# A decoder block on one core: the queries of five kv groups by seven block products in place of eight

## The chip, the cores and the metric

The kernel runs on one core of a Trainium2 chip. The metric is the device time of one execution in microseconds: the median of three runs is 661.36 us (659.74 to 665.2). Engines are named as in the profile: PE (TensorE, matmuls; PEld its weight loads), DVE (VectorE), ACT (ScalarE), POOL (GpSimd) and SP, whose queue issues all the DMAs.

## The reference

The input `x` is 8 batches of 128 tokens of 512 values. Three blocks follow, each added to `x`; `ln` is a layer norm without weights.

```python
# 32 query heads in 8 kv groups of 4, head size 128, causal
q = (ln(x) @ w_q).reshape(B, S, 8, 4, 128)       # w_q: 512 x 4096
k = (ln(x) @ w_k).reshape(B, S, 8, 128)          # w_k, w_v: 512 x 1024
v = (ln(x) @ w_v).reshape(B, S, 8, 128)
p = softmax(where(causal, einsum("bqhgd,bkhd->bhgqk", q, k) * scale, -inf))
x = x + einsum("bhgqk,bkhd->bqhgd", p, v).reshape(B, S, 4096) @ w_o
# cross attention to a context of 128 rows, whose rows are keys and values
...
# gated feed-forward, 512 -> 1376 -> 512; weights are 4-bit numbers with scales and zeros
x = x + (silu(h @ Wg) * (h @ Wu)) @ Wd           # h = ln(x)
```

## The kernel before

**Numbers.** Almost every operand of a matmul is a pair of F16 tiles, a high part and a remainder. `split` makes them: ACT casts the high part, another engine (DVE from PSUM, POOL from SBUF) subtracts it. A product (`mm3`, lines 158 to 164) is three matmuls: high by high, high by remainder, remainder by high.

**Tiles.** The 1024 tokens are two halves of 512. `hT[part][half]` is ln(x) transposed: four blocks (`k`) of 128 rows of the contraction by 512 tokens. A head's queries for one half are thus 4 x 3 = 12 matmuls of 512 columns into a PSUM bank, `ps_q` (`proj_q`), then split into `qh` and `ql`.

**Steps.** The main loop runs over 64 steps, a kv group `g` and a batch `b` each. A step contains:

- `att_s` of the next step: 12 score matmuls of 64 or 128 columns into `ps_sc` (tag `s`); on DVE four custom reductions that add the mask and find the row maximum; on ACT four exponentials with row sums; then `rec` on DVE and POOL, two scalings of `s` on POOL, the split into `pb` (ACT casts, POOL subtracts), and a transposing DMA `pt<-pb` on SP.
- `proj_piece`: a quarter of the projections of the unit (a group's half) that comes next.
- `att_o` of the step before: 12 matmuls of 512 columns into `ps_o`, added to `xr` by DVE.
- `att_v`: five matmuls of 256 columns into `ps_at` from `pt`, then the split into `ah` and `al`.

**Weights.** They arrive in F32. `fetch_w*` issues the DMA into a raw tile; `sumsq` sums squares on ACT; `scales` makes a scale with a tiny matmul (`ps_n`) and DVE; `convert` multiplies on POOL in place, casts on ACT and subtracts on POOL. A table `todo` says after which step each of these is written.

**Quantized weights.** `nf` are three F16 tiles for the feed-forward weights, filled from step 8 on by `dequant`, in 35 pieces: DMAs of the numbers (`qr`) and of the zeros (`zi`, from a DRAM copy `zd`), two DVE instructions each. The pool `deqp` holds their temporaries, and those of the prologue.

**Order.** `begin` (the prologue) is written in order by hand (`in_order`), as are parts of the tail. In between, the framework's scheduler places the instructions on each engine by its own model; an engine then executes its queue in that order. So which tile waits for which follows from the program, but the order around the change is a result of the build. PSUM has eight banks, two each for the tags `j` (projections), `s`, `a` and `o`.

Of the kernel before, what the change touches and what calls it, by code (L numbers as in the profile page):

```python
# [17 lines left out]
P = 128  # L18
HQ = 64
B = 8  # L20
# [33 lines left out]
def tile_decoder(  # L54
# [34 lines left out]
    masks = []  # L89
    for k in range(2):  # L90
        m = const.tile([P, (k + 1) * HQ], F32, name=f"mask{k}")
        nc.gpsimd.memset(m, 0.0)
        for p0 in (0, HQ):
            part = m[p0 : p0 + HQ, :]
            nc.gpsimd.affine_select(
                part,
                part,
                [[-1, (k + 1) * HQ]],
                ALU.is_ge,
                NEG,  # L100
                base=k * HQ,
                channel_multiplier=1,
            )
        masks.append(m)
# [80 lines left out]
    BANKS = {"j": 2, "s": 2, "a": 2, "o": 2}  # L185
# [9 lines left out]
    qp = pool("q", 5)  # L195
    rawp = pool("raw", 2)
    hp = pool("hT", side="right")
# [18 lines left out]
    def fetch_wq(g, pieces=((0, GH),)):  # L216
        src = wq[:, g * TH : (g + 1) * TH].rearrange("(kt p) d -> p kt d", p=P)
        raw_t["q", g] = raw = rawp.tile([P, KT, TH], F32, name="rawq", tag="rawq", bufs=1)
        for a, b in pieces:
            nc.sync.dma_start(raw[:, :, a * P : b * P], src[:, :, a * P : b * P])  # L220

    def fetch_wk(g):
        raw_t["k", g] = raw = rawp.tile([P, KT, P], F32, name="rawk", tag="rawk")
        nc.sync.dma_start(
            raw, wk[:, g * P : (g + 1) * P].rearrange("(kt p) d -> p kt d", p=P)
        )

    def fetch_wv(pr):
        raw_t["v", pr] = raw = rawp.tile(
            [P, KT, 2 * P], F32, name="rawv", tag="rawv", bufs=1  # L230
        )
        nc.sync.dma_start(
            raw, wv[:, pr * 2 * P : (pr + 1) * 2 * P].rearrange("(kt p) d -> p kt d", p=P)
        )
# [7 lines left out]
    def sumsq(kind, g, i, j, n=1):  # L242

        raw = raw_t[kind, g]
        if kind == "q":
            view = raw[:, :, j * P : (j + 1) * P]
# [11 lines left out]
        junk = work.tile([P, 2 * TH], BF16, name="junk", tag="junk", bufs=1)  # L258
# [105 lines left out]
    def prep_wq(g, j, direct=False):  # L364
# [3 lines left out]
        raw = raw_t["q", g][:, :, j * P : (j + 1) * P]  # L368
# [34 lines left out]

    def ln_stats(b):
# [11 lines left out]
    def ln_apply(b):  # L416
# [3 lines left out]
        h = deqp.tile([P, H], F32, name="h", tag=("qr", "zi")[b % 2], bufs=2)  # L420
# [19 lines left out]
    def h_wide(b):  # L440

        cs = slice(b * P, (b + 1) * P)
        ps = transpose4(ln_t.pop(("h", b)), "s" if b == 2 else "o")
# [15 lines left out]
    def k_wide(g):  # L459
# [13 lines left out]
        wide = h32.rearrange("p k t -> p (k t)")[:, :TH].rearrange("p (b t) -> p b t", b=HB)  # L473
# [5 lines left out]
    def h_dma(b):  # L479
# [3 lines left out]
        hb = deqp.tile([P, 2, H], F16, name="hb", tag="hb", bufs=HB)  # L483
# [16 lines left out]
    def proj_q(g, half, j, pieces=(slice(0, TH),)):  # L500

        ps = bank("j", [P, TH], "ps_q")
        if j % 2 == 0:
            q_t[g, half, j // 2] = [
                qp.tile([P, HB, 2, 2, HQ], F16, name="q" + p, tag="q" + p) for p in "hl"
            ]
        hi, lo = q_t[g, half, j // 2]
        for cs in pieces:
            proj(ps[:, cs], wq_t[g * GH + j], half, cs)
            yield  # L510
        split(
# [3 lines left out]
        )  # L515
        yield
# [12 lines left out]
    def proj_v(pr, b):  # L529
        half, bb = divmod(b, HB)  # L530
        cs = slice(bb * P, (bb + 1) * P)
        ps = bank("j", [P, 2 * P], "ps_v")
# [146 lines left out]
    def scales_load():  # L679

        rows = deqp.tile([SROWS, NFT * P], F16, name="srow", tag="srow")
# [4 lines left out]
        zt["s"] = deqp.tile([P, NFT, SROWS], F16, name="scol", tag="scol")  # L686
# [25 lines left out]
    def inter_scale():  # L712
# [16 lines left out]
        junk = work.tile([P, 2 * TH], BF16, name="junk", tag="junk", bufs=1)  # L729
# [31 lines left out]
    def zeros_load():  # L761
        zw = deqp.tile([NZ, INTER // 8], I32, name="zw", tag="zw")
# [6 lines left out]
    def zeros(es, after):  # L769
        if "z" not in zt:  # L770
            zt["z"] = deqp.tile([NZ, INTER // 8, 8], I32, name="z", tag="z")
# [11 lines left out]
    def zeros_store():  # L783

        zt["d"] = dram.tile([NZ, INTER], I32, name="zd")
        nc.sync.dma_start(zt["d"], zt["z"].rearrange("p a e -> p (a e)"))

    def dequant(m, g, c0, c1, after, pts=None):
# [11 lines left out]
        zi = deqp.tile([P, H], I32, name="zi", tag="zi", bufs=2)  # L800
# [29 lines left out]
    def begin():  # L830

        warm = const.tile([P, TH], BF16, name="warm")
        nc.vector.memset(warm, 0.0)
        psw = bank("s", [P, TH], "ps_w")
# [5 lines left out]
        fill(11)  # L840
# [10 lines left out]
        fetch_wk(1)  # L851
# [79 lines left out]
        prep_wv(0, 1, True)  # L931
        next(q[2])
# [42 lines left out]
    def c_load(b):  # L975
        raw_t["c", b] = c = xc.tile([P, H], F32, name="c", tag="c", bufs=3)
        nc.sync.dma_start(c, cx[b])

    def c_prep(b):
# [3 lines left out]
        cp = xc.tile([P, 2, H], F16, name="cp", tag="cp", bufs=B)  # L983
# [65 lines left out]
    zero = const.tile([P, P], F32, name="zero")  # L1049
    nc.gpsimd.memset(zero, 0.0)  # L1050
# [10 lines left out]
    XC = chunk_steps[-1] + 1  # L1061
# [30 lines left out]

    def h3_load(b):
# [6 lines left out]
    def proj_parts(u, j):  # L1100
# [6 lines left out]
        run(proj_q(g, half, j))  # L1107
        yield
        if projects_v(u) and j in (1, 2):
            for q in range(2):  # L1110
                run(proj_v(g // 2, half * HB + (j - 1) * 2 + q))
# [11 lines left out]
    for g in range(1, NG):  # L1123
        u0 = units.index((g, 0))
        c = HB * (u0 - 2)
        if g > 1:
            m = c - HB
            at(m, lambda g=g: fetch_wk(g))
            at(m + 1, lambda g=g: (fetch_wq(g), sumsq("k", g, 0, 0)))
            at(m + 2, lambda g=g: (sumsq("q", g, 0, 0), sumsq("q", g, 0, 1)))  # L1130
            at(m + 3, lambda g=g: (sumsq("q", g, 0, 2), sumsq("q", g, 0, 3)))
            at(m + 3, lambda g=g: (scales("q", g), scales("k", g), soft_scale(g)))
        for j in range(GH):
            at(c + j, lambda g=g, j=j: prep_wq(g, j))
# [9 lines left out]
        if g % 2 == 0:  # L1144
            c = HB * (u0 - 3)
            at(c - 2, lambda g=g: fetch_wv(g // 2))
            at(c - 1, lambda g=g: sumsq("v", g // 2, 0, 0))
# [337 lines left out]
```

## Time and profile before

| | |
|---|---|
| median of three runs | 661.36 us |
| span of the profiled execution | 659.3 us |
| PE busy | 630.6 us, 96% |
| DVE, ACT, POOL busy | 469.9, 440.4, 395.8 us |
| mean granted TensorE clock | 0.995 |
| DMA | 69.34 MB, mean 105 GB/s |

The profiled execution's own time is known as its span, from the first to the last instruction; it lies within 0.1% of the fastest of the runs, and 2.1 us below their median. PE's busy time is the union of its instructions, which overlap; it doesn't say how many more would fit. Of the loop's 64 steps the profile shows one `rec` on POOL each: from 33.5 us (the first) to 529.1 us (the last). The steps of the groups come before the feed-forward's chains (`ps_c`), which begin among the last attention steps.

### The profile page before, as it was taken

Reading aid. Unit: us, or ns where it says so; the run is one execution under the profiler, and the core shown is the slowest. Engines: PE = TensorE matmul, PEld = TensorE weight load, DVE = VectorE, ACT = ScalarE, POOL = GpSimd, SP = SyncE. Lnnn points to the kernel's source line nnn. Section 1 sums busy time; section 2 is a strip of 40 time slices with the busy share of each in tenths; the row PEclk is TensorE's granted clock in tenths of the full one; section 3 lists DMA queues with packets and bytes.
Section 4 is the critical chain, followed back from the end, with each engine's and each line's share of the span. In section 5 each row is a group of like instructions: output and inputs, shape, how many; then the busy total and the mean of one; then the engine's idle time right before and its main releaser. Section 6 shows DMA issues by size and latency. Waiting matters only on the chain.

```text
span 659.3 us, 12426 instructions
## 1 busy us (share of the span) xinstructions
PE 630.6 (96%) x3992; PEld 341.9 (52%) x3992; DVE 469.9 (71%) x1474; ACT 440.4 (67%) x1238; POOL 395.8 (60%) x586
## 2 busy tenths in 40 slices
PE   8789999899999999999999999899998988999996
PEld 5455545455655555565555565456554444445443
DVE  6845786656767776675778565677776768988986
ACT  5676677465758574666677565976566578867674
POOL 7757497664747795556588597663576247622521
PEclk9999999999999999999999999999999999999998
DMA  9277244945553755455547514242544243112002
GB/s 316 54 174 146 84 46 133 229 105 158 121 157 80 192 130 153 109 152 140 144 112 163 149 37 120 46 103 57 90 76 70 41 86 55 22 27 65 1 1 64
DMA packets 117773, 69.34 MB, mean 105 GB/s; under 512 B 84190, under 2 KB 100593, under 8 KB 117708
## 3 DMA queue, kind: packets, MB, share of 16 engines
q1 hardware_dynamic: 117708, 68.55, 43.7%
q8 instruction: 31, 0.51, 0.3%
q14 instruction: 34, 0.28, 0.1%
HBM read 42.12 MB, written 2.20 MB: 67 GB/s over the span
## 4 chain that ended last, share of the span: by engine, by line
PE 56%; POOL 13%; DMA 10%; DVE 8%; issue 7%; ACT 5%; SPq 1%; DVEq 0%; POOLq 0%; ACTq 0%
PE ps_c L1184 6%; PE ps_c L1185 6%; PE ps_o L164 5%; PE ps_o L162 5%; PE ps_o L163 5%; PE ps_q L163 5%; PE ps_q L162 5%; PE ps_q L164 5%; DMA pt<-pb 3%; DMA rawq<-in_L_attn_w_q_dram 3%; POOL pb L119 3%; DMA rawo<-in_L_attn_w_o_dram 2%; POOL s L625 2%; POOL wql L119 1%; POOL rawo L356 1%
## 5 line engine op out<-in xcount | busy, mean ns | idle before, releaser
L568 ACT ACTIVATE s<-s,negm 128x64 f32<-128x64 f32 (+1 forms) x256 | 93.1, 365 | 31.6 <-DVE negm L611 31.3
L162 PE MATMUL ps_o<-woh,ah 128*128 128x512 f16 x256 | 97.1, 379 | 3.2 <-ACT ah L116 3.2
L162 PE MATMUL ps_q<-hT,wqh 128*128 128x512 f16 (+1 forms) x260 | 98.2, 378 | 1.7 <-DVE ql L119 1.7
L163 PE MATMUL ps_q<-hT,wqh 128*128 128x512 f16 (+1 forms) x260 | 98.2, 378 | 0.0
L164 PE MATMUL ps_q<-hT,wql 128*128 128x512 f16 (+1 forms) x260 | 98.0, 377 | 0.0
L164 PE MATMUL ps_o<-woh,al 128*128 128x512 f16 x256 | 96.9, 379 | 0.6 <-DVE al L119 0.6
L163 PE MATMUL ps_o<-wol,ah 128*128 128x512 f16 x256 | 97.0, 379 | 0.0
L119 POOL TENSOR_TENSOR pb<-s,pb 128x256 f16<-128x256 f32 (+1 forms) x128 | 71.7, 575 | 14.8 <-ACT pb L116 12.4
L665 DVE SCALAR_TENSOR_TENSOR xr<-ps_o,unsc,xr 128x512 f32<-128x512 f32 x64 | 47.8, 747 | 42.5 <-PE ps_o L164 41.9
L611 DVE CUSTOM_DVE_ANT_0 s<-ps_sc,mask,soft 128x64 f32<-128x64 f32 (+1 forms) x256 | 66.9, 309 | 4.3 <-PE ps_sc L164 2.0
L578 POOL TENSOR_SCALAR rec<-rec 128x4 f32<-128x4 f32 x64 | 14.8, 231 | 90.1 <-DVE rec L576 87.4
L625 POOL TENSOR_TENSOR s<-s,rec 128x128 f32<-128x128 f32 (+1 forms) x128 | 64.3, 523 | 4.5
L116 ACT CAST pb<-s 128x256 f16<-128x256 f32 (+1 forms) x128 | 43.0, 350 | 33.7 <-POOL s L625 30.0
L119 DVE TENSOR_TENSOR ql<-ps_q,qh 128x512 f16<-128x512 f32 x64 | 43.9, 686 | 28.8 <-ACT qh L116 28.6
L116 ACT CAST ah<-ps_at 128x512 f16<-128x512 f32 x64 | 37.1, 581 | 23.3 <-PE ps_at L164 10.1
L119 DVE TENSOR_TENSOR al<-ps_at,ah 128x512 f16<-128x512 f32 x64 | 43.7, 683 | 7.0 <-ACT ah L116 6.6
L568 ACT ACTIVATION_READ_ACCUMULATOR s<-s,negm 128x1 f32 x256 | 48.1, 188 | 0.0
L116 ACT CAST qh<-ps_q 128x512 f16<-128x512 f32 x64 | 36.7, 573 | 14.0 <-PE ps_q L164 12.5
L1197 DVE TENSOR_SCALAR ps_c<-ps_c,rTg 128x512 f32<-128x512 f32 (+1 forms) x56 | 40.7, 750 | 7.1 <-PE ps_c L1185 6.8
L356 POOL TENSOR_TENSOR rawo<-rawo,sco 128x512 f32<-128x512 f32 x30 | 31.4, 1053 | 22.5 <-DVE sco L312 20.3
L1195 ACT ACTIVATE ps_c<-ps_c,rTu 128x512 f32<-128x512 f32 (+1 forms) x57 | 36.3, 659 | 11.3 <-PE ps_c L1185 9.2
L164 PE MATMUL ps_sc<-k,ql 128*128 128x64 f16 (+1 forms) x256 | 42.7, 206 | 0.5 <-DVE ql L119 0.5
(243 smaller groups left out, 1728.9 us busy)
## 6 DMA issues: line engine op xcount, KB each, us to landing
rawq<-in_L_attn_w_q_dram SPq DMA_DIRECT2D x8, 1024.0 KB
rawo<-in_L_attn_w_o_dram SPq DMA_DIRECT2D x8, 1024.0 KB, 6.0
zi<-zd SPq DMA_DIRECT2D x26, 256.0 KB, 4.1
vd<-v SPq DMA_DIRECT2D x64, 64.0 KB, 2.6
qr<-_L_ffn_down_qweight_dram SPq DMA_DIRECT2D x10, 256.0 KB
xr<-in_x_dram SPq DMA_DIRECT2D x8, 256.0 KB, 7.7
rawk<-in_L_attn_w_k_dram SPq DMA_DIRECT2D x8, 256.0 KB, 4.5
rawv<-in_L_attn_w_v_dram SPq DMA_DIRECT2D x4, 512.0 KB
```

The lines of the kernel that those rows point to most:

```text
L116: a = nc.scalar.copy(hi, src)
L119: b = (lo_eng or nc.vector).tensor_tensor(lo, src, hi, ALU.subtract)
L162: nc.tensor.matmul(ps, lh, rh, start=start and i == 0, stop=False)
L163: nc.tensor.matmul(ps, lh, rl, start=False, stop=False)
L164: nc.tensor.matmul(ps, ll, rh, start=False, stop=stop and i == n - 1)
L568: exp = nc.scalar.activation(v, v, AF.Exp, bias=negm[:, j : j + 1], scale=-1.0, accum_out=sums[:, j : j + 1],)
L611: nc.vector.tensor_tensor_reduce(view, flat(ps, cols[j]), masks[j // 2], soft_t[g][:, j % 2 : j % 2 + 1], BIG, ALU.add, ALU.min, negm,)
L625: mul = nc.gpsimd.tensor_tensor(v, v, rec[:, 2 * k : 2 * k + 2].unsqueeze(2).to_broadcast([P, 2, (k + 1) * HQ]), ALU.mult,)
L665: return nc.vector.scalar_tensor_tensor(xr[b], ps, unsc_t[g], xr[b], ALU.mult, ALU.add)
L1184: nc.tensor.matmul(ps, lh, rh, start=r == 0, stop=False, skip_group_check=r > 0)
L1185: nc.tensor.matmul(ps, lh, rl, start=False, stop=True, skip_group_check=r > 0)
L1197: nc.vector.tensor_scalar(ps, ps, sc, None, ALU.mult)
```

## The change

The queries of kv groups 2 to 6 are computed for two heads and both halves at once. With the contraction cut in two (`low`: blocks 0 and 1, `high`: blocks 2 and 3), the tokens in two halves and the weights in two heads, this is a product of 2 x 2 blocks. It is done with seven block products in place of eight (Strassen's scheme in Winograd's form). A block product is 2 x 3 = 6 matmuls of 512 columns.

- `t_part` (after steps 3 to 6) forms four sums of the token blocks once, with DVE in F32, and splits them into `tT` (`T` in the profile).
- `fast_prep` does the weights of a pair of heads in four parts: two products with scales, four sums of 128x256 on POOL, and the splits of `X`, `Y` (a half), `Z0` and `Z1`.
- `fast_q` multiplies in four stages, one a step (two a step for group 2). Sums of products stay in PSUM: `u` (`ps_qu`) is begun by an ACT copy of half of `c11` and then added to by three products; `c12` is begun by a DVE sum. `s5` is a copy of `m5` in SBUF.
- PSUM: the tag `s` has one bank, the freed one is `b`, for `u`. From group 2 on, `proj_v` uses the tag `o`. The feed-forward's chains go around `j`, `s`, `o`, `j`, `b`, `o`.
- Query weights come in two DMAs of two heads; there are two such raw tiles in place of one double. Fetches, squares and scales have other steps. Key and value raw tiles share one buffer.
- The prologue's temporaries (warm-up tile, layer-normed tokens, first key weights, scales, zeros) and `t_part`'s are views of `nf` (`lent`), not tiles of `deqp`. Zeros are kept as F16.
- `XC`, the step from which the context is loaded, goes from 43 to 47; there are fewer buffers for it (`c` 3 to 2, `cp` 8 to 6).

```diff
-    BANKS = {"j": 2, "s": 2, "a": 2, "o": 2}
+    BANKS = {"j": 2, "s": 1, "a": 2, "o": 2, "b": 1}
...
-    def fetch_wq(g, pieces=((0, GH),)):
-        src = wq[:, g * TH : (g + 1) * TH].rearrange("(kt p) d -> p kt d", p=P)
-        raw_t["q", g] = raw = rawp.tile([P, KT, TH], F32, name="rawq", tag="rawq", bufs=1)
-        for a, b in pieces:
-            nc.sync.dma_start(raw[:, :, a * P : b * P], src[:, :, a * P : b * P])
+    def fetch_wq(g, pairs=(0, 1)):
+        for p in pairs:
+            c0 = g * TH + p * 2 * P
+            raw_t["q", g, p] = raw = rawp.tile([P, KT, 2 * P], F32, name="rawq", tag="rawq")
+            nc.sync.dma_start(
+                raw, wq[:, c0 : c0 + 2 * P].rearrange("(kt p) d -> p kt d", p=P)
+            )
...
+    tT = tp.tile([P, 2, 4, 2, TH], F16, name="T")
+
+    def t_part(i):
+        low, high = slice(0, 2), slice(2, KT)
+        one, two = tmp32
+        hh, hl = hT[0][1], hT[1][1]
+        if i == 0:
+            nc.vector.tensor_tensor(one, hh[:, low, :], h32[:, low, :], ALU.subtract)
+            nc.vector.tensor_tensor(one, one, hl[:, low, :], ALU.add)
+            src = one
+        elif i == 1:
+            nc.vector.tensor_tensor(two, hh[:, high, :], one, ALU.subtract)
+            nc.vector.tensor_tensor(two, two, hl[:, high, :], ALU.add)
+            src = two
+        elif i == 2:
+            nc.vector.tensor_tensor(one, two, h32[:, low, :], ALU.subtract)
+            src = one
+        else:
+            nc.vector.tensor_tensor(one, h32[:, high, :], two, ALU.subtract)
+            src = one
+        split(tT[:, 0, i], tT[:, 1, i], src, nc.gpsimd)
...
+    def fast_units(key, raw, kts=slice(0, KT)):
+        n = raw.shape[1]
+        hi = wqp.tile([P, KT, P], F16, name="wqh", tag="wqh")
+        lo = wqp.tile([P, KT, P], F16, name="wql", tag="wql")
+        s_w[key] = hi, lo
+        a, b = split(hi[:, KT - n :, :], lo[:, KT - n :, :], raw, nc.gpsimd)
+
+    def fast_prep(g, p, part):
+        raw = fast_raw(g, p)
+        a, b = slice(0, 2), slice(2, KT)
+        if part < 2:
+            j = 2 * p + part
+            mine = raw[:, :, part, :]
+            wide = sc_t["q", g][:, j : j + 1].unsqueeze(2).to_broadcast([P, KT, P])
+            issue_after(nc.gpsimd.tensor_tensor(mine, mine, wide, ALU.mult), pace["mul"])
+            fast_units((g, p, "XY"[part]), mine if part == 0 else mine[:, b, :])
+        elif part == 2:
+            a11, a12, a21, a22 = raw[:, a, 0, :], raw[:, b, 0, :], raw[:, a, 1, :], raw[:, b, 1, :]
+            tt = nc.gpsimd.tensor_tensor
+            issue_after(tt(a22, a21, a22, ALU.add), pace["mul"])
+            tt(a21, a11, a21, ALU.subtract)
+            tt(a11, a22, a11, ALU.subtract)
+            tt(a12, a12, a11, ALU.subtract)
+        else:
+            fast_units((g, p, "Z0"), raw[:, :, 0, :])
+            fast_units((g, p, "Z1"), raw[:, :, 1, :])
+
+    def fast_q(g, p):
...
+        m5 = bank("j", [P, TH], "ps_q5")
+        term(m5, Z1, 2, summed(0), True)
+        s5 = work.tile([P, TH], F32, name="s5", tag="s5", bufs=1)
+        nc.scalar.copy(s5, m5)
+        c11 = bank("j", [P, TH], "ps_q1")
+        term(c11, X, 0, tok(0, first), True)
+        u = bank("b", [P, TH], "ps_qu")
+        nc.scalar.copy(u, c11)
+        yield
+        term(c11, X, 2, tok(0, last), False)
+        put_q(g, 0, 2 * p, c11)
+        term(u, Z0, 0, summed(1), False)
+        c12 = bank("j", [P, TH], "ps_q2")
+        nc.vector.tensor_tensor(c12, u, s5, ALU.add)
+        yield
+        term(u, Z1, 0, summed(2), False)
+        nc.vector.tensor_tensor(s5, u, s5, ALU.add)
+        term(c12, Z0, 2, tok(1, last), False)
+        put_q(g, 1, 2 * p + 1, s5)
+        put_q(g, 1, 2 * p, c12)
+        yield
+        term(u, Y, 2, summed(3), False)
+        put_q(g, 0, 2 * p + 1, u)
         yield
...
+    FAST = range(2, NG - 1)
...
+    for g in FAST:
+        for p in range(2):
+            base = 8 * g - 9 + 4 * p
+            where = [base, base + 1, base + 2, base + 3]
+            if g == FAST[0]:
+                where = [11 + 2 * p, 11 + 2 * p, 12 + 2 * p, 12 + 2 * p]
...
+        if g in FAST:
+            for p in range(2):
+                to = 8 * g - 13 + 4 * p if g > FAST[0] else 4 + 4 * p
+                up = to - (2 if g == FAST[0] else 3 if (g, p) == (FAST[0] + 1, 0) else 4)
+                both = 2 * p, 2 * p + 2
+                at(up, lambda g=g, p=p: fetch_wq(g, (p,)))
+                at(to - 2, lambda g=g, p=p: sumsq("q", g, 0, 2 * p))
+                at(to - 1, lambda g=g, p=p: sumsq("q", g, 0, 2 * p + 1))
+                at(to - 1, lambda g=g, both=both: scales("q", g, both))
+                for part in range(4):
+                    at(to + part, lambda g=g, p=p, part=part: fast_prep(g, p, part))
```

`put_q` is the end of `proj_q` (the split into `qh` and `ql`) as a function of its own; `term` issues the six matmuls of a block product into a bank.

## The prediction

> **What bounds the kernel now.** I read four views, in this order: the page's busy shares, the timeline of TensorE in a steady stretch, the table of stretches, and the groups by shape.
>
> ```profile
> PE 630.6 (96%) x3992; PEld 341.9 (52%) x3992; DVE 469.9 (71%) x1474; ACT 440.4 (67%) x1238; POOL 395.8 (60%) x586
> ```
>
> TensorE is busy for 96% of the span. But the mean time of a matmul is not its price. The timeline shows it:
>
> ```profile
> 211.40 0.38 PE L164 MATMUL ps_o<-woh,al 128*128 128x512 f16 x1
> 211.62 0.38 PE L164 MATMUL ps_q<-hT,wql 128*128 128x512 f16 x1
> 211.83 0.38 PE L162 MATMUL ps_q<-hT,wqh 128*128 128x512 f16 x1
> 212.05 0.38 PE L163 MATMUL ps_q<-hT,wqh 128*128 128x512 f16 x1
> ```
>
> Each lasts 0.38 us, but the next starts 0.216 us later: they overlap. A removed 512-column matmul is worth 0.216 us.
>
> The stretches (columns: us of the stretch, then busy us of PE, PEld, DVE, ACT, POOL with counts, granted clock, DMA share, GB/s) show where TensorE has no gaps and how full the others are there:
>
> ```profile
> 200.00:220.00 20.00, 20.00 (x135) 10.63 (x133) 14.22 (x49) 15.70 (x51) 17.86 (x26) 1.00 0.38 92
> 380.00:400.00 20.00, 19.94 (x142) 11.86 (x141) 12.86 (x44) 12.74 (x42) 19.41 (x26) 1.00 0.19 40
> 400.00:420.00 20.00, 17.40 (x114) 9.03 (x113) 9.85 (x45) 14.26 (x47) 10.66 (x19) 1.00 0.38 103
> 520.00:540.00 20.00, 18.70 (x98) 8.75 (x97) 13.04 (x30) 10.73 (x19) 9.42 (x13) 1.00 0.31 59
> ```
>
> In the groups' steps TensorE is the bound, but POOL has bursts of 17.9 and 19.4 us in 20. The latter is just carried; after it TensorE stands idle for 2.6 us. The prices on POOL (mean ns after the comma):
>
> ```profile
> L119 POOL TENSOR_TENSOR pb<-s,pb 128x256 f16<-128x256 f32 x64 | 44.6, 696 | 13.2 <-ACT pb L116 10.8 <-DVE negm L611 0.8
> L625 POOL TENSOR_TENSOR s<-s,rec 128x256 f32<-128x256 f32 x64 | 40.6, 634 | 0.0
> L119 POOL TENSOR_TENSOR wql<-rawq,wqh 128x512 f16<-128x512 f32 x28 | 32.5, 1167 | 0.8 <-ACT wqh L116 0.8
> L356 POOL TENSOR_TENSOR rawq<-rawq,scq 128x512 f32<-128x512 f32 x28 | 29.2, 1048 | 16.0 <-DVE scq L312 15.7 <-DVE sb L283 0.3
> ```
>
> **Removed: matmuls.** A pair of heads took 2 heads x 2 halves x 12 = 48 matmuls of 512 columns; seven products of 6 are 42. Ten pairs (five groups, two pairs each) save 60, and the built order has them: 696 instead of 756. 60 x 0.216 = 13.0 us, all in a stretch where TensorE has no gaps. Five more column sums at 0.03 us are nothing.
>
> A page speaks against even this. The Trainium skill, "TensorE: Matmul & The Clock Gate", section "Back-to-back issue gap", gives about 131 ns for a matmul of N=512 in a stream of weight loads and matmuls; by it the saving would be 60 x 0.131 = 7.9 us. This trace has 0.216 us in just such a stream, so the trace decides.
>
> **Added: POOL.** Before, a pair cost POOL two products (1.048) and two remainders (1.167), 4.4 us. Now: two products, four sums of 128x256, three remainders of 128x512 and one of 128x256 (0.70, the `pb` row). No row has a sum of two f32 tiles of 256: half a product is 0.52, and the POOL row of `ob` (128x256, two tiles in) has 0.83. I take 0.67, between the two rows shown above of that size. A pair then costs 2.10 + 2.68 + 3.50 + 0.70 = 9.0 us, 4.6 more; ten pairs 46. The four sums of tokens in `t_part` add four remainders of 128x1024, at 2.15 each by the slope of the `pb` rows (454 ns for 128, 696 for 256): 8.6. POOL goes from 396 to 450 us.
>
> What is late next: POOL is one queue. It makes the weights' low parts and the probabilities' low parts (`pb`), and `pb` must still go through the transposing DMA before `att_v`. So I compared the built orders of POOL and TensorE between points tied to each other: from the `rec` of step 20 (it needs that step's scores) to the last remainder of group 4's first pair (its first matmul, `m5`, needs it).
> - POOL: 4 `rec` x 0.23, 4 + 4 scalings (0.41, 0.63), 3 + 3 `pb` (0.45, 0.70), 8 products x 1.05, 8 remainders x 1.17, one of 0.70, 4 sums x 0.67 = 29.7 us.
> - TensorE: 97 matmuls of 512 (21.0), 20 of 256 (0.109 each, 2.2), five steps' scores (0.51 each, 2.6) = 25.8 us.
> - From a step's last score matmul to `rec` the trace never has less than 2.3 us.
>
> So TensorE must wait 29.7 + 2.3 - 25.8 = 6.2 us there, whatever else goes well. The `pb` of step 25, with 2.8 us more from `pb` to the first `att_v` matmul (least in the trace), gives nearly the same, 5.8: it is one delay, not two. Group 6's first pair, from step 36 on, has 28.8 + 2.3 - 25.0 = 6.1. The same comparison for the kernel before never comes nearer than 0.2 us to a wait, and at its bursts 2.4. Together +12.3 us. With sums at 0.52 and 0.83 it is 11.1 and 13.6; with all POOL rows 5% cheaper (its busy stretches come out up to 7% under the sum of means) 9.3.
>
> **Added: ACT and DVE.** A pair adds two PSUM copies (0.58) and 768 columns of casts (1.0) to ACT, 22 us in all, with 4.2 for `t_part`; and two PSUM sums (0.75, the `ps_c` row) to DVE, 15 us, with six 128x1024 differences. These have no row: twice 0.70 (`ps_q`) is 1.4, twice 1.05 (`wvl`, two SBUF inputs) 2.1; I take 1.5, so 9. Over 280 us of steps that brings either from about 68% to about 77% busy. The four hand-overs of a pair (two copies, two sums) lie between stages a step (7 us) apart, and TensorE has 2.6 us of `ps_o` and more between. Group 2 has two stages in one step and half that cover. If every hand-over there were bare, 8 x 0.7 = 5.6; I take +1.5, range 0 to 6.
>
> The page "SBUF — State Buffer", section "Who interferes with whom", says that a DVE instruction with two SBUF inputs shuts out a GpSimd one that reads SBUF. The six differences and ten `ql` out of `s5` are of that kind: 6 x 1.5 + 10 x 0.69 = 16 us, an estimate by that page of what POOL could lose more. In this trace the DVE row of `cp`, two SBUF inputs, spreads from 0.75 to 1.68 us, so something holds it; that POOL pays in full no row shows, and I leave it out of the sum.
>
> **Moved.** `c_load` to `c_prep` come four steps later, 50 to 57 in place of 46 to 53. A `c_prep` is 1.0 us of small DVE work and 0.83 for `cp`, and ACT pays 1.5; four now fall where cross-attention starts and TensorE already loses 6.7 us of 80 (480 to 560 us). Between 0 and 4 x 1.8 = 7: I take +2. The prologue: `rawq` comes in two DMAs, and the chain waits for it from 3.1 to 9.7 us; at best half of 6.5 is gained, 3.3. Against it, the scores have one bank: the next scores wait for four reductions (1.5 us), which a step covers, but not the first three, whose `rec` come 1.7 to 2.2 us apart; up to 3 lost. I take -1. The zeros in F16 halve `zi`'s bytes, off the path: TensorE never waits for it.
>
> **Sum.** 659.3 - 13.0 + 12.3 + 1.5 + 2 - 1 = 661.1 us of span. The median of the three runs, 661.4, is 2.1 above the profiled span, so 663.2: I say 663. Its own range: 655 to 671.
>
> **Rivals.**
> - Faster: POOL isn't late. For it: from 380 to 400 us POOL ran at 19.4 of 20 and TensorE kept 19.94; a queue can be full and harm nothing. Against it: the counts above leave no room. If POOL's rows shrink in a dense queue and 2 us are left at each of the two places: 659.3 - 13.0 + 4 - 1 + 0.5 + 2.1 = 652.
> - Slower: the weights' fetch falls behind. `rawq` has two half-size buffers; a late last remainder keeps one, SP's fetch of the next pair but one waits for it, and the squares (`sumsq`) two steps later stand at the head of ACT's queue with exponentials, `ah` and `qh` behind. Two steps are 14 us, landing took 6.5 to 7.7, so it decides from about 6.5 us of POOL's lateness, and I computed 6.2. For it: before, ACT waited up to 3.4 us for `rawo` so, and TensorE lost the 2.6 us at 413. Against it: SP's order places these fetches with a step to spare. Six later pairs at 2 us: 663 + 12 = 675.
> - The matmuls are worth their 0.379 us: 60 of them 22.7, and with half the wait 645. The start times above speak against it. That the change leaves the products as they were is excluded by the count of 696.
>
> **Numbers.** POOL's wait takes the gain back: 0.43; faster rival 0.29; slower rival 0.25; dear matmuls 0.03. A measurement of this kernel can tell about 1% (6.6 us) from no change: below 654.7 is faster, above 668 slower. Of the first case 0.33 lies within and 0.10 above. So faster 0.32, same 0.33, slower 0.35; range 648 to 677.
>
> **What would show it.** Right: 512-column query matmuls 60 fewer, still 0.216 us apart; POOL near 450 us; idle TensorE of some 6 us shortly before the matmuls of groups 4 and 6 on summed tokens (`T`), ended by POOL's `wql` or by `pt`. Wrong: POOL's sums well off 0.67; TensorE without gaps from 100 to 400 us (the faster rival); ACT's `junk` waiting for `rawq` several times (the slower one); or waits ended by `s5`, `ps_qu` or `ps_q2`, for which I have only 1.5 us.

## The result, and the profile after

The changed kernel takes 688.56 us (686.05 to 691.51) against 660.82 for the kernel before: a ratio of 1.041, 95% interval 1.037 to 1.046, or 27 us slower. The forecast was 663 us, 648 to 677.

The page of the changed kernel: its span, busy shares, and the chain of waits by engine.

```profile
span 684.7 us, 12496 instructions
...
PE 626.8 (92%) x3937; PEld 337.5 (49%) x3937; DVE 509.0 (74%) x1521; ACT 460.1 (67%) x1282; POOL 464.1 (68%) x647
...
POOL 30%; PE 29%; issue 11%; ACT 10%; DVE 10%; DMA 8%; SPq 0%; POOLq 0%; DVEq 0%; ACTq 0%
```

The same line of the kernel before, from its chain of waits:

```profile
PE 56%; POOL 13%; DMA 10%; DVE 8%; issue 7%; ACT 5%; SPq 1%; DVEq 0%; POOLq 0%; ACTq 0%
```

TensorE has less to do and the kernel is longer: in the chain that ended last TensorE's share falls from 56 to 29%, and POOL's rises from 13 to 30%. The groups by shape of the changed kernel give the prices (busy us, then mean ns):

```profile
L117 POOL TENSOR_TENSOR pb<-s,pb 128x256 f16<-128x256 f32 x64 | 46.6, 728 | 16.2 <-ACT pb L114 13.1 <-DVE sb L289 1.6 <-DVE rs L1141 1.0
...
L117 POOL TENSOR_TENSOR T<-nfg,T 128x1024 f16<-128x1024 f32 x4 | 8.5, 2128 | 0.0
...
L604 POOL TENSOR_TENSOR rawq<-rawq 128x256 f32<-128x256 f32 x10 | 8.1, 805 | 0.2
...
L605 POOL TENSOR_TENSOR rawq<-rawq 128x256 f32<-128x256 f32 x10 | 7.5, 747 | 0.2
```

The four sums cost 0.75 to 0.81 us, 0.78 in the mean, where 0.67 was forecast; `pb` went from 0.70 to 0.73.

To see where the time went I cut each trace at the first reduction (`s<-ps_sc` on DVE) of some steps. Idle is the time from one matmul's start to the next beyond its undisturbed spacing (0.216 us for 512 columns, 0.109 for 256, less for fewer), so it holds half-speed stretches too. Each cell is time, then idle, in us; the last column counts the prologue and the tail too; the last four rows are experiments told below.

| steps | 0-4 | 4-12 | 12-20 | 20-28 | 28-36 | 36-44 | 44-52 | 52-60 | idle in all |
|---|---|---|---|---|---|---|---|---|---|
| before | 38.5, 4.5 | 58.1, 2.9 | 65.1, 0.0 | 51.5, 0.2 | 70.5, 0.6 | 51.4, 0.0 | 67.3, 3.8 | 67.7, 3.7 | 34.6 |
| changed | 36.2, 10.3 | 66.6, 3.7 | 74.7, 1.1 | 50.3, 7.7 | 76.7, 3.4 | 53.1, 9.6 | 70.1, 3.2 | 64.2, 11.3 | 71.5 |
| p_mm | 35.6, 2.5 | 58.9, 2.9 | 63.5, 0.0 | 50.6, 1.5 | 68.0, 0.6 | 50.9, 0.8 | 67.3, 5.1 | 67.3, 5.6 | 38.8 |
| p_pool | 37.2, 11.0 | 65.4, 2.6 | 73.6, 0.0 | 48.7, 6.0 | 73.9, 0.7 | 50.5, 7.0 | 68.3, 1.4 | 64.6, 11.7 | 60.8 |
| p_all | 30.0, 4.2 | 65.0, 2.1 | 73.6, 0.0 | 49.2, 6.5 | 74.3, 1.1 | 52.6, 9.1 | 68.6, 1.6 | 65.1, 12.2 | 56.6 |
| p_heavy | 36.3, 10.3 | 67.1, 3.8 | 72.5, 6.8 | 50.0, 7.0 | 74.0, 8.5 | 53.2, 9.8 | 75.1, 8.1 | 63.9, 11.0 | 86.8 |

Idle time grew by 37 us, in three kinds of place: steps 0 to 4, where the sums of tokens are made; steps 20 to 28 and 36 to 44, the octets that hold no projections of `v`; and steps 52 to 60.

A cell's time less its idle time is what TensorE's matmuls take there, and these have moved. Steps 12 to 20 hold 73.6 us of them for 65.1 before, with almost no idle time; steps 20 to 28, 36 to 44 and 52 to 60 hold 42.6, 43.5 and 52.9 for 51.3, 51.4 and 64.0. The first of these became 9.6 us longer, while steps 20 to 28 and 36 to 44, with 8.7 and 7.9 us less to multiply, take 50.3 and 53.1 us for 51.5 and 51.4: their time went into idle.

Two stretches of the second kind, about steps 23 to 27 and 39 to 43, in the table of stretches of the changed kernel (busy us of PE, PEld, DVE, ACT, POOL):

```profile
231.00:261.00 30.00, 23.62 (x167) 12.54 (x165) 23.31 (x87) 24.86 (x85) 29.40 (x43) 1.00 0.53 131
...
357.00:393.00 36.00, 27.89 (x179) 14.28 (x178) 26.91 (x84) 24.81 (x83) 33.61 (x50) 0.96 0.52 133
```

The same steps of the kernel before:

```profile
209.00:244.00 35.00, 34.94 (x225) 18.32 (x224) 26.62 (x82) 24.73 (x81) 30.45 (x44) 1.00 0.60 143
331.00:366.00 35.00, 35.00 (x226) 18.53 (x225) 26.60 (x87) 25.67 (x84) 30.74 (x44) 1.00 0.57 126
```

POOL is full to 98 and 93%, TensorE to 79 and 77%. Before, TensorE had no gap and POOL stood at 87 and 88%. What TensorE waits for, in the waits of the changed kernel (us in total, times, longest):

```profile
PE ps_o L162 <- DVE al L117: 7.7, 8, 2.3
PE ps_at L789 <- DMA pt<-pb: 6.6, 10, 1.8
PE ps_v L160 <- DVE ql L117: 5.2, 3, 2.5
PE ps_q L160 <- DVE v L689: 3.1, 1, 3.1
PE ps_sc L160 <- DVE negm L752: 2.9, 4, 0.9
```

Of these only `pt` comes from POOL directly (4.2 us before). The others end on DVE; what made DVE late in each is not shown by this view.

### The profile page after: what moved, and what is told of

Read it like the earlier page. It is cut to its first block, busy times and chain, and to the rows that moved or that the text cites. A ratio compares the mean times of both kernels' runs of the same rounds, so it can differ in the third digit from the quotient of the medians.

```text
span 684.7 us, 12496 instructions
## 1 busy us (share of the span) xinstructions
PE 626.8 (92%) x3937; PEld 337.5 (49%) x3937; DVE 509.0 (74%) x1521; ACT 460.1 (67%) x1282; POOL 464.1 (68%) x647
## 4 chain that ended last, share of the span: by engine, by line
POOL 30%; PE 29%; issue 11%; ACT 10%; DVE 10%; DMA 8%; SPq 0%; POOLq 0%; DVEq 0%; ACTq 0%
PE ps_c L1362 6%; POOL pb L117 6%; PE ps_c L1363 5%; POOL s L766 5%; POOL wol L117 3%; POOL wql L117 3%; DMA pt<-pb 3%; DMA rawo<-in_L_attn_w_o_dram 3%; POOL rawo L362 3%; PE ps_o L162 2%; PE ps_o L160 2%; PE ps_o L161 2%; ACT s L709 2%; ACT junk L266 2%; POOL rec L719 1%
## 5 line engine op out<-in xcount | busy, mean ns | idle before, releaser
L117 POOL TENSOR_TENSOR pb<-s,pb 128x256 f16<-128x256 f32 (+1 forms) x128 | 77.2, 618 | 20.0 <-ACT pb L114 16.8
L766 POOL TENSOR_TENSOR s<-s,rec 128x128 f32<-128x128 f32 (+1 forms) x128 | 65.4, 532 | 2.9
L114 ACT CAST pb<-s 128x128 f16<-128x128 f32 (+1 forms) x128 | 42.7, 348 | 32.4 <-POOL s L766 29.1
L719 POOL TENSOR_SCALAR rec<-rec 128x4 f32<-128x4 f32 x64 | 16.9, 265 | 70.0 <-DVE rec L717 55.9
L117 POOL TENSOR_TENSOR wql<-rawq,wqh 128x512 f16<-128x512 f32 (+1 forms) x48 | 51.9, 1093 | 4.6 <-ACT wqh L114 4.5
L162 PEld LDWEIGHTS <-al 128*128 128x128 f16 x256 | 25.2, 98 | 40.9 <-DVE al L117 11.2
L160 PE MATMUL ps_sc<-k,qh 128*128 128x64 f16 (+1 forms) x256 | 39.7, 207 | 3.8 <-DVE negm L752 2.9
L160 PE MATMUL ps_q<-hT,wqh 128*128 128x512 f16 (+1 forms) x100 | 37.6, 376 | 4.8 <-DVE v L689 3.1
L160 PE MATMUL ps_v<-wvh,hT 128*128 128x256 f16 x128 | 35.4, 277 | 6.3 <-DVE ql L117 5.2
L161 PE MATMUL ps_sc<-k,qh 128*128 128x64 f16 (+1 forms) x256 | 41.0, 206 | 0.0
```

The lines of the kernel that those rows point to most:

```text
L114: a = nc.scalar.copy(hi, src)
L117: b = (lo_eng or nc.vector).tensor_tensor(lo, src, hi, ALU.subtract)
L160: nc.tensor.matmul(ps, lh, rh, start=start and i == 0, stop=False)
L161: nc.tensor.matmul(ps, lh, rl, start=False, stop=False)
L162: nc.tensor.matmul(ps, ll, rh, start=False, stop=stop and i == n - 1)
L766: mul = nc.gpsimd.tensor_tensor(v, v, rec[:, 2 * k : 2 * k + 2].unsqueeze(2).to_broadcast([P, 2, (k + 1) * HQ]), ALU.mult,)
```

## The experiments

In the expectations, theory A is that POOL's queue is late because of what the scheme adds; rival B that the re-arrangement costs (score bank, banks of `v`, lent temporaries); rival C that the hand-overs and the added ACT and DVE work cost; rival D that the order which the build gave each engine decides; theory E that the saved matmuls covered other chains. Ratios are to the kernel before, measured beside each, with 95% intervals; us are the ratio's distance from 1, times 660.5.

### Parts undone, each kernel in the order of its own build

**no_fast.** `FAST` is empty and `t_part` is not called.

```diff
-    FAST = range(2, NG - 1)
+    FAST = range(0)
```

> This is the changed kernel with the list of groups that use seven products emptied and without the sums of tokens: all queries by eight products again, everything else of the change kept (one score bank, v in the banks of tag o, the lent temporaries, rawq in two DMAs, the context four steps later). Theory A (POOL's queue is what TensorE waits for, because of the sums, remainders and products that the seven-product scheme adds): POOL is back near 396 us busy, TensorE has 60 more matmuls, and the time is 661 us within 3. Rival B (the re-arrangement itself costs: fewer score banks, v in other banks, a denser prologue): 672 to 690, with TensorE's waits still on negm, v and al. Half and half: about 667.

668.87 us, 1.013 (1.009 to 1.016), 8.3 us slower than before: both theories have a share. The re-arrangement alone costs something, and the seven products, with 13.0 us fewer matmuls by spacing, add 19 to it.

**no_sums and sums_dve.**

```diff
-            issue_after(tt(a22, a21, a22, ALU.add), pace["mul"])
...
+            pass                             # no_sums
...
-            tt = nc.gpsimd.tensor_tensor
+            tt = nc.vector.tensor_tensor     # sums_dve
```

> The changed kernel without the four sums of weight blocks on POOL in each pair (part 2 of fast_prep is empty, so the blocks multiplied are not the sums; the count of matmuls, casts, remainders and transfers stays). It takes 40 x 0.78 = 31 us of work from POOL. Theory A: the stalls of the groups' steps (some 24 us more than before) mostly go: 665 to 671. Rival B (re-arrangement): not below 684. Rival C (the hand-overs of the seven products, s5, ps_qu, ps_q2, and DVE with two SBUF inputs): not below 682.

> The changed kernel with the four sums of weight blocks of each pair on DVE in place of POOL; the result is the same. POOL 464 down to some 433 us, DVE 509 up to some 535. Theory A: 668 to 676, since DVE at 79% has more room than POOL's bursts. Rival B: 685 to 690. Rival C (DVE with two SBUF inputs and POOL hold one another up, or DVE is late itself): 685 or more, and POOL's remainders get dearer (above 1.25 us for wql of 512).

673.82 us, 1.020 (1.016 to 1.024), and 677.00 us, 1.026 (1.022 to 1.030): 14 and 10 us faster than the changed kernel. Near theory A; but both have new orders, which mattered below.

**no_tpart and no_T.** `t_part` isn't called; in no_tpart a memset on DVE fills `tT`, in no_T `summed` returns blocks of `hT`.

```diff
-            return tT[:, 0, i], tT[:, 1, i]
+            return tok(1, (first, last)[i % 2])      # no_T
```

> The changed kernel without the four sums of token blocks after steps 3 to 6: the tile T is zeroed once at the start on DVE, and its products are made with zeros. POOL loses four remainders of 2.13 us, DVE six differences, ACT four casts, all before step 11. TensorE waited 9.3 us more than before in the first 80 us. Theory A: most of that goes: 678 to 682. Rival (the prologue's loss comes from the lent temporaries and the one score bank): 686 to 689.

> The changed kernel without the sums of tokens and without the tile T: the products that use T use blocks of hT instead, nothing is zeroed. Against the run no_tpart, which had a zeroing of some 3 us on DVE at the start. In the trace of the changed kernel TensorE lost 10.3 us between the first and the fifth rec, without the sums 3.2. Theory A (those sums hold up POOL, ACT and DVE where the first scores, v and k are made): 680 to 683. Rival (a later order takes it back, as in no_tpart, 687): 685 to 689.

687.15 us, 1.041 (1.037 to 1.045), and 687.51 us, 1.040 (1.035 to 1.045). Both missed: nothing is gained, although the idle time between the first and the fifth `rec` fell from 10.3 to 3.2 and 3.8 us. Later stretches took it back in their new orders.

**pool_even.** No sums, no sums of tokens, no remainders of `Z0` and `Z1`.

```diff
-            fast_units((g, p, "Z0"), raw[:, :, 0, :])
...
+            for i in range(2):
+                hi = wqp.tile([P, KT, P], F16, name="wqh", tag="wqh")
+                s_w[g, p, f"Z{i}"] = hi, s_w[g, p, "X"][1]
+                nc.scalar.copy(hi, raw[:, :, i, :])
```

> The changed kernel with POOL's work brought back to that of before while the seven products stay: no sums of weight blocks, no remainders of Z0 and Z1 (the low part of X stands in for theirs) and no sums of tokens (blocks of hT stand in for T). The values of these queries are not the reference's; matmuls, copies out of PSUM, casts and transfers stay as in the changed kernel, so it has 60 matmuls fewer than no_fast (668.9 us) at the same POOL load, 13.0 us of TensorE. Theory A (only POOL's added work is late): 655 to 659. Rival C (the hand-overs of the seven products and their ACT and DVE work cost too): 662 to 670. If POOL hardly mattered: above 672.

669.48 us, 1.013 (1.010 to 1.017), POOL at 397.9 us: as much as no_fast, which has 60 matmuls more. So POOL's load is not the whole.

**nf_s2 and b_xc47.**

```diff
-    BANKS = {"j": 2, "s": 1, "a": 2, "o": 2, "b": 1}
+    BANKS = {"j": 2, "s": 2, "a": 2, "o": 2}          # nf_s2, on no_fast
...
-    XC = chunk_steps[-1] + 1
+    XC = chunk_steps[-1] + 5                          # b_xc47, on the kernel before
```

> no_fast with two score banks again (s 2, no bank b; the feed-forward's chains use s where they used b). no_fast is 7.5 us slower than before: 2 at the start, 4 where the context is prepared (between rec 52 and 60), 1.6 in the tail. If the one score bank costs this: 661 to 664. If it doesn't: 667 to 670.

> The kernel before with one edit: the context is loaded and prepared four steps later (from step 47 in place of 43). My prediction gave this 2 us, between 0 and 7; no_fast loses 4 us more than before between rec 52 and 60. If the later context is that loss: 664 to 666. If not: 660 to 662.

nf_s2: 678.36 us, 1.026 (1.023 to 1.030), 9.0 us slower than no_fast with a bank more for the scores: neither expectation. Its idle time grew by nearly 5 us in steps 44 to 52 and 7.5 in the tail. It is inconclusive on the bank, and shows what a new order can do. b_xc47: 664.87 us, 1.006 (1.003 to 1.009): the later context costs 4 us (2 to 6), and idle time in steps 52 to 60 goes from 3.7 to 9.1 us, about as in no_fast (8.5). The profiled execution was the slowest of its eight, 669.55 us, so these 5.4 us are more than the median shows.

**v_act.** A version: the products with scales on ACT.

```diff
-            wide = sc_t["q", g][:, j : j + 1].unsqueeze(2).to_broadcast([P, KT, P])
-            issue_after(nc.gpsimd.tensor_tensor(mine, mine, wide, ALU.mult), pace["mul"])
+            sc = sc_t["q", g][:, j : j + 1]
+            issue_after(nc.scalar.activation(mine, mine, AF.Copy, scale=sc), pace["mul"])
```

> The changed kernel with the two products with scales of each pair on ACT in place of POOL (one ACT instruction of 128x512 each), order as built; the result is the same. POOL 464 to some 443 us, ACT 460 to some 472. Theory A, and DVE and POOL holding one another up: 676 to 682. If ACT's queue is as tight as POOL's: 686 to 692.

684.67 us, 1.038 (1.032 to 1.043): 2.6 us better than the changed kernel, within the intervals; POOL 444.8, ACT 471.9 us. A miss.

### One thing cut at a time, with the order kept

A rebuilt kernel has another order, so the next kernels are built twice: first unmodified, and then with the cut (`_MOD[0]` true) and each engine's queue chained in the order of the first build. Only the second runs. The instructions stay in place; those cut get small. No kernel ran with its order kept and nothing cut; p_hand, at 688.51 us, comes closest to that.

**p_sums, p_pool.**

```diff
+            w = slice(0, 4 if _MOD[0] else P)
-            a11, a12, a21, a22 = raw[:, a, 0, :], raw[:, b, 0, :], raw[:, a, 1, :], raw[:, b, 1, :]
+            a11, a12, a21, a22 = raw[:, a, 0, w], raw[:, b, 0, w], raw[:, a, 1, w], raw[:, b, 1, w]
...
+        if _MOD[0] and key[2][0] == "Z":                # p_pool alone
+            nc.gpsimd.memset(lo[:, ks, :], 0.0)
```

> The changed kernel with every engine's queue in exactly the order of the changed kernel's build (pinned), and only the four sums of weight blocks of each pair cut from 128x256 to 128x8 elements on POOL (the queries' values change). Runs no_sums and sums_dve had orders of their own. Theory A (POOL's queue is late): 664 to 672, as no_sums (673.8) or better. Rival D (the time hangs on the order that each build happens to get, not on the sums): 680 or more.

> As p_sums, order pinned, and the remainders of Z0 and Z1 are replaced by zeroing the low parts on POOL too: POOL's load is about that of before, with the seven products, hand-overs, casts and sums of tokens kept. Theory A: 655 to 661, the 13 us of TensorE mostly visible. Rival C (hand-overs and the added ACT and DVE work cost as well, as pool_even at 669.5 suggests): 664 to 671.

p_sums: 685.49 us, 1.037 (1.033 to 1.042), only 3 us less. One event hides part of it: a DVE instruction held for 7.67 us at 413 us (last section), which the changed kernel hasn't; steps 44 to 52 are 4.3 us longer with it. p_pool: 678.59 us, 1.027 (1.023 to 1.031). POOL is at 429.7 us (a cut sum still takes 0.26, a zeroing 0.52), so 34 us less of POOL give 9.6 us. Rival D looks strong after p_sums; p_pool is far above both expectations. About the two stretches shown above, in p_pool:

```profile
226.00:256.00 30.00, 25.25 (x174) 13.16 (x172) 24.26 (x81) 23.94 (x81) 26.14 (x43) 1.00 0.58 130
350.00:386.00 36.00, 30.48 (x201) 15.92 (x200) 27.84 (x87) 26.88 (x89) 31.30 (x53) 1.00 0.54 134
```

POOL is at 87% in both, as in the kernel before, but TensorE at 84 and 85%, where it had no gap before. So POOL's load is only a part of what TensorE waits for there.

**d_sums.** The reverse of p_sums, and the edit is shown against it: the order comes from the build with cut sums, the work is whole.

```diff
-            w = slice(0, 4 if _MOD[0] else P)
+            w = slice(0, P if _MOD[0] else 4)
```

> The changed kernel with all its work, but each engine's queue in the order that the build gives when the four sums are cut to 128x8 elements. no_sums was 15 us faster than the changed kernel, p_sums (same cut, order kept) only 3. If the other 12 are the order (rival D): 675 to 680, at full work. If the order of a build fits only its own work: 686 or more.

698.67 us, 1.057 (1.053 to 1.062), worse than either. Rival D falls in this form: with all the work, the order built for less of it is 11 us worse than the changed kernel's own. The 11 us between no_sums and p_sums then need both, the removed work and an order fitted to its absence, beside the event above.

**p_hand.** ACT's copy into `u` and DVE's sum into `c12` on 4 columns; the next products start anew.

```diff
-        nc.scalar.copy(u, c11)
+        nc.scalar.copy(u[:, cut], c11[:, cut])
...
-        nc.vector.tensor_tensor(c12, u, s5, ALU.add)
+        nc.vector.tensor_tensor(c12[:, cut], u[:, cut], s5[:, cut], ALU.add)
```

> The changed kernel, order pinned, with two hand-overs of each pair cut to 128x4 elements: ACT's copy of c11 into u and DVE's sum into c12 (the products that followed them start their banks anew, so the queries' values change). Waits on them stay, but last some 0.2 in place of 0.6 to 0.7 us, and ACT and DVE lose 12 us of work in all. Prediction's term for all hand-overs was 1.5 us (0 to 6). Theory A: 684 to 688. Rival C: 676 to 682.

688.51 us, 1.045 (1.039 to 1.051): nothing is gained. Rival C falls for these two; the hand-overs through `s5` were not cut.

**p_T.** `t_part` cut; its matmuls stay.

```diff
+        w = slice(0, 4 if _MOD[0] else TH)
...
-            nc.vector.tensor_tensor(one, hh[:, low, :], h32[:, low, :], ALU.subtract)
+            nc.vector.tensor_tensor(one[:, :, w], hh[:, low, w], h32[:, low, w], ALU.subtract)
...
+            nc.gpsimd.memset(tT[:, 1, i], 0.0)
```

> The changed kernel, order pinned, with the sums of tokens cut: DVE's differences and ACT's casts to 4 columns, POOL's remainders replaced by zeroing; products with T use that zero tile. In the trace of no_T TensorE's 6.5 us between the first and the fifth rec were gone, but the time stayed (687.5), with other orders later. If the token sums cost what that stretch shows: 680 to 683. If later waits take it back even at the same order: 686 to 689.

680.11 us, 1.030 (1.026 to 1.034): 7.7 us. The stretch from 40 to 60 us, first of the changed kernel, then of p_T:

```profile
40.00:60.00 20.00, 13.81 (x85) 7.75 (x83) 14.33 (x36) 16.99 (x46) 19.75 (x20) 0.91 0.35 57
```

```profile
40.00:60.00 20.00, 17.87 (x126) 10.96 (x125) 11.42 (x46) 16.46 (x55) 16.28 (x23) 1.00 0.41 95
```

With the sums of tokens POOL is busy 19.75 us of 20 and TensorE 13.8, at a granted clock of 0.91; without them TensorE does 126 matmuls in place of 85.

**p_all.** The cuts of p_pool, p_hand and p_T together.

> The changed kernel, order pinned, with all of these cut at once: the sums of weight blocks, the remainders of Z0 and Z1 (zeroed), the sums of tokens, and the two hand-overs of a pair. What stays of the change are 60 fewer matmuls, 768 columns of casts a pair on ACT, the re-arrangement and the order. If added work is the cause (theory A with C): 655 to 661. If the pieces add up as measured one by one (10 for POOL, some 6 for the tokens, under 1 for the hand-overs): 671 to 673, and the rest is order and re-arrangement.

672.07 us, 1.017 (1.013 to 1.021): 16 us less, close to the sum of the pieces. What stays is 11 us above the kernel before, with 60 matmuls fewer, and its idle time is still 6.5 and 9.1 us in steps 20 to 28 and 36 to 44. These two take 1.1 us less than before with 16.5 us less to multiply, while steps 12 to 20 have no idle time and are 8.5 us longer, by the matmuls that came there. So with the added work cut, where the matmuls stand is a strong candidate for what stays; no run moved them back.

**p_mm.** The kernel before, in its order, with 60 of its matmuls cut short and nothing added.

```diff
+            if _MOD[0] and 2 <= g < NG - 1 and half and j % 2:
...
+                    n = TH if k < 2 else 4
```

> The kernel before, its order pinned, with six of the 48 query matmuls of each pair of heads in groups 2 to 6 cut from 512 to 4 columns (second half, odd head, blocks 2 and 3; those queries' values change): the matmuls that the change saves, with nothing added. If TensorE's spacing is the price, as predicted: 60 x (0.216 - 0.03) = 11 us less, 649 to 651. Rival E (these matmuls also cover the chain from scores to pt and from ps_at to ah and al, so other waits take their place): 653 to 659.

654.06 us, 0.990 (0.987 to 0.993): 6.5 us (4.4 to 8.7) of the 11.2 that spacing gives, as theory E had it. By stretch (12 matmuls cut, 2.2 us, in each of five octets) steps 12 to 20 and 28 to 36 give 1.6 and 2.5, steps 20 to 28, 36 to 44 and 52 to 60 only 0.9, 0.5 and 0.4. Steps 0 to 4 are 2.9 us shorter too, but nothing was cut there: the profile of the kernel before has 3.4 us at half the granted clock at 48 us, that of p_mm has none.

**p_light and p_heavy.** The changed kernel with 80 query matmuls cut to 4 columns, of groups 4 and 6 or of groups 3 and 5.

```diff
+                n = 4 if _MOD[0] and (g, p) in ((4, 0), (6, 0)) else TH     # p_heavy: (3, 0), (5, 0)
...
-                mm(ps, wh, rl, start=False, stop=False, skip_group_check=not start)
+                mm(ps[:, :n], wh, rl[:, :n], start=False, stop=False, skip_group_check=no)
```

> The changed kernel, order pinned, with 80 of the 84 query matmuls of the first pairs of groups 4 and 6 cut from 512 to 4 columns (those queries' values change): they run in steps 25 to 27 and 40 to 42, where TensorE has idle time. If TensorE's spacing is the price there too: 80 x 0.187 = 15 us less, 672 to 675. If the chain of a step (scores, reductions, exponentials, pb, pt) sets the time of these sparse steps (theory E): 0 to 5 us less, 683 to 689.

> The same with the first pairs of groups 3 and 5, whose matmuls run in steps 15 to 19 and 31 to 35, where TensorE is not idle. By TensorE's spacing and by theory E alike: 672 to 677. If the time hangs on POOL's queue everywhere (theory A in its strong form): 682 or more.

691.21 us, 1.046 (1.041 to 1.050), and 687.74 us, 1.042 (1.036 to 1.047). Taking 15 us of matmuls from the changed kernel gains nothing in all in either place. In p_light that is near theory E's forecast: steps 20 to 28 and 36 to 44 take 50.2 and 53.2 us, as in the changed kernel. In p_heavy it was not: steps 12 to 20 and 28 to 36 get 2.2 and 2.7 us shorter, not 7.5 each. Both lose 5 us in steps 44 to 52, with the held DVE instruction again, and have more stretches at half clock, nine and six for three (last section). So in the changed kernel TensorE's matmuls are worth nothing where it is idle and a third of their spacing where it isn't; what stands behind them there was not isolated.

No version ran faster than the kernel before, except p_mm, which leaves work out. A version with the second sum in PSUM in place of `s5` was not tried.

## Why the prediction was wrong

The forecast was some 25 us short. Three of its steps failed by 6 to 8 us each: the credit for the saved matmuls, the sums of tokens, which have no cost in it, and the re-arrangement. Some 8 us more have no known place.

- **Saved matmuls, -13.0: the failed premise.** Count and spacing were right. "All in a stretch where TensorE has no gaps" was read as "each is worth its spacing". p_mm measures a little over half (6.5 of 11.2), and least in the octets without `v` and in steps 52 to 60. A full engine isn't an engine with nothing just behind it; what stands behind it, this run doesn't tell.
- **POOL, +12.3: a cost of that order (p_pool, 9.6), but not as a sum of two waits.** The idle time came at the places named, a few steps later (23 to 27 and 39 to 44 in place of 20 to 24 and 36 to 40), with POOL full. But steps 20 to 28 and 36 to 44 hold 17.1 us more idle time than before, not 12.3, and p_pool brings them only 4.2 us of time and leaves most of the idle time; its other gains are spread over the groups. POOL's order was compared with TensorE's, while DVE and ACT were priced as loads, not as queues that can be late. The waits that ended on `al`, `ql`, `v` and `negm` have no term.
- **POOL's prices:** 464 us, not 450. Sums at 0.78 for 0.67 are 4.4 us of it.
- **The shared port, left out of the sum (up to 16 us).** Instructions do get longer, on both engines: added up against the shortest tenth of their kind (tiles and shape), POOL's last 29 us longer, 12 before, and DVE's 55, 39 before. POOL's longest, 1.4 to 2.0 us in place of 0.4 to 1.0 between 43 and 55 us, stand beside the differences of tokens. How much of the 27 us this makes, and that the port is its cause, no run shows by itself.
- **Sums of tokens: no term of their own.** "The prologue: -1" took what `rawq` and the score bank do; the 8.5 us of remainders and 9 of differences were counted as load only. They fall where POOL is full (19.75 us of 20): p_T, 7.7 us for POOL's, DVE's and ACT's part together. By a little this is the largest single miss that a run shows.
- **Hand-overs, +1.5 (0 to 6):** p_hand finds nothing for the two of four that it cuts.
- **The re-arrangement, +2 for the later context and -1 for the prologue and the score bank:** no_fast, with an order of its own, measures 8.3 (6.1 to 10.5). The later context is 4 of it (b_xc47), inside its range of 0 to 7; the rest has no term.
- **The slower rival, the weights' fetch:** its sign did not come: ACT's `junk` waited for `rawq` twice, as before, 5.8 us for 3.0. But its waits for all loads are 32 us, 13 before (`rawo` 8.5 for 6.0, the context 7.1 for 1.2), and no run tests what these cost. The faster rival is excluded by the time, and by p_pool, which gains from a lighter POOL.

The pieces: +8.3 (no_fast) - 6.5 (p_mm) + 9.6 (p_pool) + 7.7 (p_T) = 19.1 of 27.3, an estimate, since no_fast has another order and p_mm is the old kernel. The other 8 are not placed: orders, 768 columns of casts a pair, POOL's work that p_pool leaves, the waits for loads, and the queries of both halves made early (steps 51 to 55 have no query matmul left, and 6.8 us of idle time for 1.1 before) could each hold them. The last fits best with where p_all loses its time, but was not tested. Nor did any run split the 8.3 of no_fast beyond the 4 of the later context.

## What to carry to other kernels

Before you credit removed work on the busiest engine, shorten that work in the old kernel with its order kept and look at what the time does: here 11 us of matmuls were worth 6.5 in the old kernel, and 15 in the new one 0 where TensorE was idle and 5 where it wasn't. When a scheduler orders the queues, a part left out comes with a new order (no_tpart and no_T: 0 us; nearly the same cut at the old order, p_T: 7.7), so pin the order when you ask what a part costs. And work moved onto an engine that has bursts is priced at its bursts, not by its mean share: POOL, busy for 68% of the changed kernel, was at 98 and 93% in two stretches where TensorE stood idle.

## What the runs showed of the hardware

**A DVE instruction can last until POOL's queue has a break, but seldom does.** The timeline of DVE in p_heavy:

```profile
413.74 0.42 DVE L692 SCALAR_TENSOR_TENSOR v<-ps_v,v 128x256 f16<-128x256 f32 x1
414.39 7.67 DVE L117 TENSOR_TENSOR ql<-s,qh 128x512 f16<-128x512 f32 x1 [0.23 <-ACT qh L114]
421.99 0.41 DVE L692 SCALAR_TENSOR_TENSOR v<-ps_v,v 128x256 f16<-128x256 f32 x1
```

and of POOL at that time:

```profile
414.20 1.16 POOL L117 TENSOR_TENSOR wql<-rawq,wqh 128x512 f16<-128x512 f32 x1
415.31 0.98 POOL L769 TENSOR_TENSOR s<-s,rec 128x128 f32<-128x128 f32 x2
416.24 1.05 POOL L362 TENSOR_TENSOR rawo<-rawo,sco 128x512 f32<-128x512 f32 x1
...
419.24 1.16 POOL L117 TENSOR_TENSOR wol<-rawo,woh 128x512 f16<-128x512 f32 x1
420.35 1.16 POOL L117 TENSOR_TENSOR wql<-rawq,wqh 128x512 f16<-128x512 f32 x1
```

The subtraction, both of whose inputs are in SBUF, lasts 7.67 us and ends half a microsecond after POOL's row of instructions does; the same split out of PSUM takes 0.68. Behind it stand `v`, `ql` and `al`, and TensorE is idle for 3.3 us. p_light and p_sums have it too, at 7.68 and 7.67. This is no rule: the same instruction of the changed kernel, begun with 7.6 us of such a row ahead, took 1.52 us, and another with 30 us ahead 1.26. It need not be a large instruction; in d_sums, with POOL busy throughout:

```profile
108.26 4.94 DVE L289 CAST sb<-ssq 128x2 bf16<-128x2 f32 x1
```

In the changed kernel none is that long, but 24 DVE instructions last over 0.7 us more than the shortest tenth of their kind, 11 in the kernel before. Its groups of DVE by shape:

```profile
L117 DVE TENSOR_TENSOR ql<-ps_q,qh 128x512 f16<-128x512 f32 x44 | 30.0, 682 | 12.4 <-ACT qh L114 12.4
...
L953 DVE TENSOR_SCALAR qi<-qr,sh 128x512 int32<-128x512 int32 x26 | 19.6, 753 | 0.0
...
L117 DVE TENSOR_TENSOR ql<-s,qh 128x512 f16<-128x512 f32 x10 | 11.4, 1142 | 5.1 <-ACT qh L114 5.1
```

`qi` was 628 ns before, and has nothing to do with the change. ACT's rows don't stretch: `ah` takes 579 ns, 581 before. The Trainium skill, "SBUF — State Buffer", section "Who interferes with whom", has a lock on a port pair that DVE and GpSimd share: in DVE's two-port modes whoever issues first holds it for the whole instruction, a DVE instruction with two SBUF inputs contends with a GpSimd one that reads SBUF, and ACT never waits. The prediction cited it for POOL's loss alone. In p_heavy the subtraction waited through eight of POOL's instructions; that the lock is the cause, no run isolates.

**TensorE can run at half speed after an idle stretch of some 3 us, and need not.** The timeline of the changed kernel:

```profile
51.44 0.19 PE L162 MATMUL ps_sc<-k,ql 128*128 128x64 f16 x1
54.75 0.38 PE L160 MATMUL ps_q<-hT,wqh 128*128 128x512 f16 x1 [3.11 <-DVE v L689]
54.96 0.38 PE L161 MATMUL ps_q<-hT,wqh 128*128 128x512 f16 x1
...
56.07 0.63 PE L162 MATMUL ps_q<-hT,wql 128*128 128x512 f16 x1
56.50 0.63 PE L160 MATMUL ps_q<-hT,wqh 128*128 128x512 f16 x1
```

The starts are 0.216 us apart after the wait, and 0.43 from 55.6 us on, for 8 matmuls: 1.65 us lost. The granted clock shows it as half for 3.4 us. The changed kernel has three such stretches before its end and the kernel before one, at most 5.1 and 1.7 us lost; p_light has nine. The same 3.1 us wait stands at 55 us in p_hand, p_pool and p_light, and no half clock follows it there. In the kernel before the one at 48 us follows waits of 0.5, 1.1 and 0.4 us. So a single wait does not decide it. The Trainium skill, "TensorE: Matmul & The Clock Gate", section "What's actually happening", names an idle window of some 3.4 us ahead of the slow clock; here it came after 3.1 us, and at 390 us after two waits of 1.1 and 2.4 us with matmuls between them.
